# A two-layer image kernel: five statistics tiles asked for first, the next image's statistics two units later, one load of layer 1 behind the last unit's reciprocal

## The chip, the cores and the metric

The kernel runs on one core of one Trainium2 chip. The metric is the device time of one execution in microseconds (us); the median of three runs is shown. A profile is one further execution taken by the hardware profiler. Its engines are PE (TensorE, matmuls; PEld is its weight loads), DVE (VectorE), ACT (ScalarE), POOL (GpSimd) and SP (SyncE). SP and POOL issue the DMA transfers.

## The reference

The input `x` is 2 images of 128 channels, 256 x 256 pixels, f32. Each of two layers adds a branch to its normalised input:

```
x = x + L0(gn(x))     # windowed attention
x = x + L1(gn(x))     # convolutions
gn(v): per image, 32 groups of 4 channels: (v - mean) / sqrt(var + 1e-5)
L0: qkv = W_qkv x; q in 8 x 8 windows, k and v in 12 x 12 windows around them, 4 heads of 32
    softmax(q k / sqrt(32) + relative height and width logits + mask) v, then W_out
    (the mask leaves the keys whose row and column distances are even)
L1: t3 = depthwise 3 x 1 (full 5 x 1 convolution of x)
    t4 = x at columns -2, 0, +2 summed with w4 to 8 channels;   result = t4 * t3
```

The mean and variance of `gn` run over a whole image and four channels, so layer 0 cannot begin before the whole first image has been read once, and layer 1 normalises with statistics of layer 0's result.

## The kernel before

**Statistics of image 0.** `attention_fast` reads image 0 in tiles of 8 rows (1024 KB, name `f_sx`, six buffers) and runs `bn_stats` on VectorE, four per tile (line 128), with `bn_aggr` after every eight tiles (line 136). Three tiles are asked for ahead of the constants (`first = 3`), the first of them in four pieces of 2 rows; then come five constants, `wq_nat` and `relT`, and then the other 27 tiles, each as a buffer comes free (line 302). The last two of the 32 row groups come through `load_rows` as `f_raw` (10 rows, 1280 KB). The mean and the inverse deviation follow, and then the attention begins. Every transfer of SP waits for the eighth before it to have landed, since the transfers share eight completion semaphores in turn.

**Attention.** The work runs in units `u`; a strip `k` is 8 rows of an image (32 strips an image, 64 in all), and each strip has two units, `r` = 0 and 1, for the window rows' two parities: 128 units. A unit issues biases (L591), scores (L608), exponentials (L618), the next unit's keys (L411), coefficients (L502, L511, L515), `attend` (L634, with the reciprocals of line 640 and the products of line 643, three of each), the transposes (L654), values (L524) or the next two units' queries (L474, L476), and the projection (L411), whose result is added to the input (L670) and stored as `x1` (L674). The order in which each engine gets its instructions is the order in which the code is written (`manual_schedule`), across all five engines, SP too. `bring` and `bring_top` copy the new value rows into the window buffers `f_vt` by SP transfers (L554, L558, L561; L571, L575, L578).

**Statistics of image 1** are taken while image 0's attention runs: `stats_at` says in which unit how many rows' `bn_stats` are run, `load_next` asks for the next group of rows at the end of `attend`, behind the first reciprocal of the unit (`seen["output"]`). The one buffer of these rows (`sx`) is also the buffer of `f_top`, the top rows of an image's first strip; `f_top` is read by `bring_top` in unit 0.

**Layer 1** is a generator, `convolutions_fast`. Its first five pieces are called from the attention's last units: at the start of unit 124, at the start of unit 126, after the keys in unit 126, at the start of unit 127, and after `attend` in unit 127. `load_rows1(b, s)` asks for the rows of a strip (640 KB, line 823, and 384 KB of the strip below, line 825). `start_strip` normalises a strip (L836, L839, L840 on ScalarE), `row_sums` makes sums and differences on VectorE (L886, L890), `unfold` makes the 8-channel part (L899, copies L909 and L910, then five small SP transfers L913), `top_row` is `a_first` (L919). After these comes the loop over 64 strips, in which `vertical` (a_c, a_d, a_e, a_o) and the products run.

A load is put behind an instruction by a helper inside `attention_fast`, which adds a dependency by hand.

Of the kernel before, what the change touches and what calls it, by code (L numbers as in the profile page):

```python
# [184 lines left out]
        return self.done[name][:2]  # L185


def attention_fast(tc, io, x1_d, norm, st_x, st_y, tags, ends, weights, both, layer1):

    nc = tc.nc  # L190
    x = io["x"]
    NB, _, H, _ = x.shape
    NS = H // 8
    NU = 2 * NB * NS
    with ExitStack() as l0:
# [42 lines left out]

        raws, norms, qs, cfs, pts, ots, rcs, ons, x1s = ({} for _ in range(9))

        def after(load, ins):
            tc.add_manual_dep(
                load.ins, ins.ins.name,
                mybir.DependencyInfo(mybir.DependencyClass.Sync, mybir.DependencyReason.DATA),
                reason="a load that follows an instruction of the unit",
            )

        def load_rows(k, behind=None):

            b, s = divmod(k, NS)  # L250
            t = rawp.tile([P, 10, W], F32, tag="raw", name=f"f_raw_{k}")
            n = min(10, H - 8 * s)
            load = nc.sync.dma_start(t[:, 0:n, :], x[b, :, 8 * s : 8 * s + n, :])
            if behind:
                after(load, behind)
            raws[k] = t

        with ExitStack() as setup:
            sp = setup.enter_context(tc.tile_pool(name="f_setup", bufs=6))
            first = 3  # L260

            def statistics(i, t):
                norm.chunk(st_x[0], 4 * i, t)
                if i % 8 == 7 and i < NS - 1:
                    norm.quarter(st_x[0], "x0", i // 8)

            ahead = []
            for i in range(first):
                t = sp.tile([P, 8, W], F32, tag="sx", name=f"f_sx_0_{i}")
                for lo in range(0, 8, 8 if i else 2):  # L270
                    hi = lo + (8 if i else 2)
                    nc.sync.dma_start(t[:, lo:hi], x[0, :, 8 * (i + 2) + lo : 8 * (i + 2) + hi, :])
                ahead.append(t)
            for t, src in constants:
                nc.sync.dma_start(t, src)
            nc.scalar.mul(wq_s, wqkvT[:, 0:P], SCALE)
            wq_nat = sp.tile([P, P], F32, tag="wq_nat", name="f_wq_nat", bufs=1)
            nc.sync.dma_start(wq_nat, io["w_q"])
            relT = sp.tile([P, 2 * NREL], F32, tag="relT", name="f_relT", bufs=1)
            nc.sync.dma_start(relT, io["relT"])  # L280
            g_rel = sp.tile([P, HEADS, 2 * NREL], F32, tag="g_rel", name="f_g_rel", bufs=1)
            for h in range(HEADS):
                pg = ps_pj.tile([P, 512], F32, tag="pj", name=f"f_pg_{h}")


                nc.tensor.matmul(
                    pg[:, : 2 * NREL], wq_nat[32 * h : 32 * h + 32, :],
                    relT[32 * h : 32 * h + 32, :], start=True, stop=True,
                )
                nc.scalar.mul(g_rel[:, h, :], pg[:, : 2 * NREL], SCALE)  # L290
            for t in range(4):
                o = 11 - 2 * t
                for t1 in range(4):
                    nc.scalar.copy(wb[:, t, t1, :, 0:6], g_rel[:, :, o : o + 11 : 2])
                o = NREL + 11 - 2 * t
                for t2 in range(4):
                    nc.scalar.copy(wb[:, t2, t, :, 6:12], g_rel[:, :, o : o + 11 : 2])
            for i, t in enumerate(ahead):
                statistics(i, t)
            for i in range(first, NS - 2):  # L300
                t = sp.tile([P, 8, W], F32, tag="sx", name=f"f_sx_0_{i}")
                nc.sync.dma_start(t, x[0, :, 8 * (i + 2) : 8 * (i + 2) + 8, :])
                statistics(i, t)
            for i in range(2):
                load_rows(i)
                statistics(NS - 2 + i, raws[i][:, 0:8])
# [11 lines left out]
        stats_at, norm_at = {}, {}  # L318
        quarter_at = {}
        for b in range(NB - 1):  # L320
            row = 0
            for i in range(NS - 3):
                n = 10 if i < 12 else 8
                stats_at[2 * (b * NS + i) + 2] = b + 1, row, n
                row += n
            for i, u in enumerate((16, 28, 44, 58)):
                quarter_at[2 * b * NS + u] = st_x, b + 1, f"x{b + 1}", i
            last = 2 * (b * NS + NS - 2)
            norm_at[last - 1] = st_x, b + 1, f"x{b + 1}"
            norm_at[last + 10] = st_y, b, f"y{b}"  # L330
# [3 lines left out]
        coming, sxs, seen = sorted(stats_at), {}, {}  # L334

        def load_next():
            if coming:
                u = coming.pop(0)
                b, row, n = stats_at[u]
                t = rawp.tile([P, 10, W], F32, tag="sx", name=f"f_sx_{b}_{row}", bufs=1)  # L340
                sxs[u] = t[:, 0:n]
                after(nc.sync.dma_start(sxs[u], x[b, :, row : row + n, :]), seen["output"])

        def input_stats(u):
            b, row, n = stats_at[u]
# [277 lines left out]
        def attend(u):  # L623
            p = pts.pop(u)
            ons[0] = on = wk.tile([P, 2, NPAIR, 32], F32, tag="on", name=f"f_on_{u}", bufs=1)
            k, r = divmod(u, 2)
            if r == 0:
                rcs[0] = wk.tile([P, 2, NPAIR, 2, 1], F32, tag="rc", name=f"f_rc_{k}")
            for lo, hi in ((0, 6), (6, 11), (11, NPAIR)):
                bank = ps_pj.tile([P, 512], F32, tag="pj", name=f"f_o_{u}_{lo}")  # L630
                po = bank[:, 0 : 66 * (hi - lo)].rearrange("p (n c d) -> p n c d", c=2, d=33)
                for n in range(lo, hi):
                    for h in range(HEADS):
                        nc.tensor.matmul(  # L634
                            po[32 * h : 32 * h + 32, n - lo], p[:, h // 2, n, h % 2],
                            vt[r][:, :, n, h], start=True, stop=True,
                        )

                rc = rcs[0][:, r, lo:hi]
                ins = nc.vector.reciprocal(rc, po[:, :, :, 32:33])  # L640
                if lo == 0:
                    seen["output"] = ins
                nc.vector.tensor_tensor(  # L643
                    on[:, :, lo:hi].rearrange("p c n d -> p n c d"), po[:, :, :, 0:32],
                    rc.to_broadcast([P, hi - lo, 2, 32]), ALU.mult,
                )
# [46 lines left out]
        with tc.manual_schedule(engines=ORDERED):  # L693
# [14 lines left out]
            for u in range(NU):  # L708
                k, r = divmod(u, 2)
                b, s = divmod(k, NS)  # L710
# [5 lines left out]
                if u in norm_at:  # L716
                    st, i, name = norm_at[u]
# [22 lines left out]
                if k % NS == NS - 2:  # L740
                    step()
                attend(u)
                if u == 0 or u in stats_at:
                    load_next()
                if more and r == 1:
                    bring(1, slots_of(k + 1))
# [21 lines left out]
                if u in quarter_at:  # L768
                    st, i, name, part = quarter_at[u]
# [29 lines left out]
def convolutions_fast(tc, io, x1_d, norm, st_y, out, weights, count_good, both):  # L799

    nc = tc.nc
    NB, _, H, _ = io["x"].shape
    NS = H // 8
    with ExitStack() as l1:
# [5 lines left out]
        def rows_buffer(i):  # L810
            t = both.sb.tile([P, 12 * 260], F32, tag=f"x{i}", name=f"xm{i}")
            xn[i] = t.rearrange("p (r w) -> p r w", w=260)
            for side in (0, 2 + W):
                nc.gpsimd.memset(xn[i][:, :, side : side + 2], 0.0)

        def load_rows1(b, s):

            if s == 0:
                pre = rawp.tile([P, 10, W], F32, tag="sx", name=f"raw1_{b}_pre", bufs=1)
                nc.sync.dma_start(pre[:, 5:8, :], x1_d[b][0][:, 0:3, :])  # L820
                raws[b, -1] = pre
            t = rawp.tile([P, 10, W], F32, tag="raw", name=f"raw1_{b}_{s}")
            nc.sync.dma_start(t[:, 0:5, :], x1_d[b][s][:, 3:8, :])
            if s + 1 < NS:
                nc.sync.dma_start(t[:, 5:8, :], x1_d[b][s + 1][:, 0:3, :])
            raws[b, s] = t
# [21 lines left out]
        def pixel_buffers():  # L848

            t = both.sb.tile([P, NPAIR * HEADS * 33], F32, tag="vn", name="t4p")  # L850
            for i in range(2):
                by_pixel.append(
                    t[:, 2 * (W + 4) * i : 2 * (W + 4) * (i + 1)].rearrange("p (r w) -> p r w", r=2)
                )
                for side in (0, 2 + W):
                    nc.gpsimd.memset(by_pixel[i][:, :, side : side + 2], 0.0)
# [8 lines left out]
        def start_strip(k):  # L865
            b, s = divmod(k, NS)
            normalise1(b, s, k, *norm.done[f"y{b}"])
# [202 lines left out]

        load_rows1(0, 0)
        yield
        load_rows1(0, 1)
        yield
        rows_buffer(0)
        start_strip(0)
        yield
        row_sums(0)
        pixel_buffers()
        yield  # L1080
        unfold(0)
        top = top_row(0)
        yield
# [655 lines left out]
```

## Time and profile before

| | us |
|---|---|
| median of 3 runs | 2878.11 (2877.47 to 2878.49) |
| the profiled execution | 2877.88 |
| its span, first to last instruction | 2875.9 |
| statistics of image 0, to the last `bn_stats` | 91.8 |
| first to last unit's biases | 115.15 to 1872.10 |
| loop of layer 1, from a_c of strip 0 | 1884.3 to the end |

| engine | busy us | share |
|---|---|---|
| PE | 2753.5 | 96% |
| DVE | 2134.2 | 74% |
| PEld | 2090.1 | 73% |
| ACT | 1506.2 | 52% |
| POOL | 640.4 | 22% |

In the profile's rows, `out<-in xN` names what an instruction writes and reads and how many there are; "<-" before an engine's or a transfer's name says for what the engine waited, and "issue" is time in which the engine waited for nothing that the profile shows. L12 is line 12 of the kernel. In the chain of work, a row is start, length (both us) and what ran. Queue q8, of kind "instruction", is the transfer of instructions to an engine. Two units, that is one strip, take 27.4 us through most of the attention.

### The profile page before, as it was taken

To read this page: it belongs to the slowest core of one execution; us is meant where nothing else is said; L and a number is where in the kernel's file an instruction comes from. 1 tells how busy PE (TensorE), PEld (TensorE's weight loads), DVE (VectorE), ACT (ScalarE), POOL (GpSimd) and SP (SyncE) were. 2 spreads that over 40 slices of the span, in tenths; PEclk is the share of its full clock that TensorE was granted. 3 is DMA by queue.
4 is the path that set the end of the run, shared out by engine and by line. 5 is a ranking of instruction groups with operands and counts; after the bars stand their busy time and mean duration, and the time that the engine had idled before them with its cause. 6 is when DMAs were issued, how large, how long until landed. Compare 5 with 4: busy or idle time off the path is not lost.

```text
span 2875.9 us, 117447 instructions
## 1 busy us (share of the span) xinstructions
PE 2753.5 (96%) x51762; PEld 2090.1 (73%) x51762; DVE 2134.2 (74%) x3601; ACT 1506.2 (52%) x2379; POOL 640.4 (22%) x2049
## 2 busy tenths in 40 slices
PE   0599999999999999999999999999999999999998
PEld 0489999999999898999999999854444444444444
DVE  8667776776677666566656665589999998999987
ACT  1344454554544545455454554556666656666654
POOL 1223323333333333333333333200000000000000
PEclk9999999999999999999999999999999999999999
DMA  9566666666666455555554455557888888888885
GB/s 390 170 189 184 194 172 183 189 165 186 178 171 165 127 149 134 143 141 133 140 141 134 140 137 144 136 153 215 215 215 220 219 214 213 218 219 212 218 217 147
DMA packets 157988, 519.74 MB, mean 181 GB/s; under 512 B 20800, under 2 KB 98080, under 8 KB 117536
## 3 DMA queue, kind: packets, MB, share of 16 engines
q1 hardware_dynamic: 148400, 446.07, 52.6%
q0 software_dynamic: 9072, 66.06, 12.3%
q8 instruction: 412, 6.75, 0.9%
q14 instruction: 104, 0.85, 0.1%
HBM read 282.68 MB, written 134.22 MB: 145 GB/s over the span
## 4 chain that ended last, share of the span: by engine, by line
PE 79%; issue 17%; POOL 1%; DMA 1%; ACT 1%; DVE 1%; SPq 0%; POOLq 0%; ACTq 0%; DVEq 0%
PE f_s L608 10%; PE f_o L634 9%; PE f_pk L411 8%; PE f_pv L524 8%; PE f_py L411 8%; PE a_o L919 6%; PE a_e L919 6%; PE f_pq L476 6%; PE f_pa L502 5%; PE f_s L591 5%; PE f_pq L474 2%; PE a_d L970 2%; PE a_c L919 1%; PE b L1012 1%; PE g L899 1%
## 5 line engine op out<-in xcount | busy, mean ns | idle before, releaser
L515 DVE TENSOR_SCALAR f_cf<-f_pa,f_keep 128x512 f32<-128x512 f32 x128 | 103.7, 810 | 539.8 <-ACT f_cf L511 539.7
L618 ACT ACTIVATE f_p<-f_s 128x512 f32<-128x512 f32 x512 | 264.4, 603 | 403.1 <-PE f_s L608 403.0
L482 ACT ACTIVATE f_q<-f_pq,f_head 128x512 f32<-128x512 f32 x512 | 303.1, 702 | 146.8 <-PE f_pq L476 146.8
L425 POOL COPY f_kt<-f_kt 128x60 f32<-128x60 f32 (+1 forms) x348 | 105.7, 340 | 1176.8 <-ACT f_kt L439 1153.1
L994 ACT ACTIVATE t<-t,w 128x1024 f32<-128x1024 f32 x127 | 145.9, 1149 | 368.0 <-DVE t L987 362.8
L402 POOL COPY f_xq<-f_xn 128x96 f32<-128x96 f32 x1024 | 333.8, 357 | 3.3 <-DVE f_xn L385 3.3
L1001 DVE SCALAR_TENSOR_TENSOR t<-t,w,t 128x1024 f32<-128x1024 f32 x254 | 326.0, 1283 | 7.3 <-ACT t L994 1.3
L608 PEld LDWEIGHTS f_s<-f_q,f_kt 64*64 64x64 f32 x17176 | 270.4, 133 | 49.5 <-issue 49.5
L608 PE MATMUL f_s<-f_q,f_kt 64*64 64x64 f32 (+1 forms) x17176 | 288.1, 221 | 0.1
L634 PE MATMUL f_o<-f_vt,f_p 128*32 128x66 f32 x16384 | 263.6, 220 | 3.4 <-issue 3.4
L1030 POOL DMA_DIRECT2D y<-f_x x63 | 54.5, 866 | 919.2 <-DVE y L1022 871.2
L411 PE MATMUL f_pk<-f_xn,f_wqkvT 128*128 128x192 f32 (+3 forms) x1496 | 258.1, 322 | 0.7 <-ACT f_kt L439 0.7
L634 PEld LDWEIGHTS f_o<-f_vt,f_p 128*32 128x32 f32 x16384 | 241.8, 108 | 12.9 <-issue 2.0
L919 PE MATMUL a_o<-xm,w1s 128*128 128x512 f32 x512 | 242.3, 595 | 4.6 <-ACT t L910 4.6
L524 PE MATMUL f_pv<-f_wqkvT,f_xn 128*128 128x128 f32 x2048 | 246.0, 279 | 0.6 <-DVE f_cf L515 0.3
L411 PE MATMUL f_py<-f_ot,f_woT 128*128 128x160 f32 (+1 forms) x1520 | 244.5, 311 | 2.0 <-DVE f_ot L654 1.8
L919 PE MATMUL a_e<-xm,w1s 128*128 128x512 f32 x512 | 240.8, 591 | 0.0
L524 PEld LDWEIGHTS f_pv<-f_wqkvT,f_xn 128*128 128x128 f32 x2048 | 233.7, 192 | 6.7 <-DVE f_cf L515 0.5
L411 PEld LDWEIGHTS f_py<-f_ot,f_woT 128*128 128x128 f32 x1520 | 228.3, 191 | 4.2 <-issue 3.7
L411 PEld LDWEIGHTS f_pk<-f_xn,f_wqkvT 128*128 128x128 f32 x1496 | 221.5, 190 | 12.5 <-issue 1.7
L476 PE MATMUL f_pq<-f_xn,f_wq_s 128*128 128x192 f32 (+1 forms) x1008 | 210.4, 331 | 0.0
L643 DVE TENSOR_TENSOR f_on<-f_o,f_rc 128x320 f32<-128x320 f32 (+1 forms) x384 | 197.2, 514 | 13.3
(150 smaller groups left out, 4660.5 us busy)
## 6 DMA issues: line engine op xcount, KB each, us to landing
f_raw<-in_x SPq DMA_DIRECT2D x62, 1280.0 KB
f_x<-f_x SPq DMA_DIRECT2D x128, 512.0 KB
y<-f_x POOLq DMA_DIRECT2D x63, 1024.0 KB, 7.9
out<-y SPq DMA_DIRECT2D x63, 1024.0 KB
f_sx<-in_x SPq DMA_DIRECT2D x46, 1024.0 KB
f_vt<-f_vn SPq DMA_DIRECT2D x172, 264.0 KB
raw<-f_x SPq DMA_DIRECT2D x64, 640.0 KB
raw<-f_x SPq DMA_DIRECT2D x62, 384.0 KB
```

Of the source, the lines that this page charges most:

```text
L402: nc.gpsimd.tensor_copy(xq[:, half, t2, 1:4, :, c].rearrange("p t r n e -> p r t n e"), xn[k % 2][:, windows, :, c, 0:3, t2:8:4].rearrange ...
L411: nc.tensor.matmul(dst[:, 512 * lo // last : 512 * hi // last], w, moving[:, n * lo // last : n * hi // last], start=True, stop=True,)
L476: nc.tensor.matmul(by_pair[:, lo:hi, 8:32], wq_s, xn[k % 2][:, lo:hi, r, c, 0:3].rearrange("p n i j -> p n (i j)"), start=True, stop=True,)
L482: nc.scalar.activation(q[:, c, :, i].rearrange("p n (j t) -> p n j t", t=4), pq.rearrange("p (n t j) -> p n j t", n=NPAIR, t=4), AF.Copy, ...
L524: nc.tensor.matmul(pv[:, P * n : P * n + P], xn[k % 2][:, 4 * g + n].rearrange("p r c i j -> p (r c i j)"), wvT, start=True, stop=True,)
L608: nc.tensor.matmul(sc[g][n // 8][64 * c : 64 * c + 64, n % 8, lo:hi].rearrange("p i x -> p (i x)"), kt[r][rows, c, NKEY * n : NKEY * n + 6 ...
L618: seen["exp", half, g] = nc.scalar.activation(pts[u][:, g, 8 * half : 8 * half + 8].rearrange("p n i x -> p (n i x)"), sc[g][half].rearran ...
L634: nc.tensor.matmul(po[32 * h : 32 * h + 32, n - lo], p[:, h // 2, n, h % 2], vt[r][:, :, n, h], start=True, stop=True,)
L643: nc.vector.tensor_tensor(on[:, :, lo:hi].rearrange("p c n d -> p n c d"), po[:, :, :, 0:32], rc.to_broadcast([P, hi - lo, 2, 32]), ALU.mult,)
L919: nc.tensor.matmul(pa[:, : n * W], w, rows, start=i == 0, stop=i == len(terms) - 1)
L994: nc.scalar.activation(t3[:, j : j + 4], t1[:, j : j + 4, :], AF.Copy, scale=w3[:, 0:1])
L1001: nc.vector.scalar_tensor_tensor(t3[:, j : j + 4], t1[:, j + tap : j + tap + 4, :], w3[:, tap : tap + 1], t3[:, j : j + 4], ALU.mult, ALU.add,
```

## The change

There are three parts. (1) Five tiles instead of three are asked for ahead of the constants, and the first comes in two pieces of 4 rows instead of four of 2. (2) The statistics of the next image begin in unit 4 instead of unit 2; there are 28 groups of rows instead of 29, and sixteen of 10 rows instead of twelve; the first load is asked for in unit 2 instead of unit 0. The last unit with statistics stays unit 58. (3) In layer 1's lead-in, the second strip's rows are asked for in the fifth piece, after `attend` of unit 127, with a dependency on that unit's first reciprocal, and no longer in the second piece; `rows_buffer(0)` (memsets on POOL) goes to the second piece, and `start_strip(0)` is alone in the third. By the built program's order, the third strip's rows move on SP from ahead of `unfold(0)`'s transfers to behind the last `x1` store. The order on TensorE and ScalarE is unchanged; on POOL two edge copies of keys go behind the memsets.

```
+def follow(tc, load, ins):
...
-            first = 3
+            first = 5
...
-                for lo in range(0, 8, 8 if i else 2):
-                    hi = lo + (8 if i else 2)
+                for lo in range(0, 8, 8 if i else 4):
+                    hi = lo + (8 if i else 4)
...
-            for i in range(NS - 3):
-                n = 10 if i < 12 else 8
-                stats_at[2 * (b * NS + i) + 2] = b + 1, row, n
+            for i in range(NS - 4):
+                n = 10 if i < 16 else 8
+                stats_at[2 * (b * NS + i) + 4] = b + 1, row, n
...
-                    seen["output"] = ins
+                    seen["output"] = weights.output = ins
...
-                if u == 0 or u in stats_at:
+                if u == 2 or u in stats_at:
                     load_next()
...
-        def load_rows1(b, s):
+        def load_rows1(b, s, behind=None):
...
-            nc.sync.dma_start(t[:, 0:5, :], x1_d[b][s][:, 3:8, :])
+            load = nc.sync.dma_start(t[:, 0:5, :], x1_d[b][s][:, 3:8, :])
+            if behind:
+                follow(tc, load, behind)
...
         load_rows1(0, 0)
         yield
-        load_rows1(0, 1)
+        rows_buffer(0)
         yield
-        rows_buffer(0)
         start_strip(0)
         yield
         row_sums(0)
         pixel_buffers()
         yield
+        load_rows1(0, 1, weights.output)
         unfold(0)
         top = top_row(0)
         yield
```

More of the change, by code (lines that the diff above doesn't have):

```diff
@@ L185, in group @@
         return self.done[name][:2]
+def follow(tc, load, ins):
+    tc.add_manual_dep(
+        load.ins, ins.ins.name,
+        mybir.DependencyInfo(mybir.DependencyClass.Sync, mybir.DependencyReason.DATA),
+        reason="a load that follows an instruction of the unit",
+    )
 def attention_fast(tc, io, x1_d, norm, st_x, st_y, tags, ends, weights, both, layer1):
@@ L239, in attention_fast @@
         raws, norms, qs, cfs, pts, ots, rcs, ons, x1s = ({} for _ in range(9))
[L241 to L246, printed above, removed]
         def load_rows(k, behind=None):
@@ L254, in load_rows @@
             if behind:
-                after(load, behind)
+                follow(tc, load, behind)
             raws[k] = t
@@ L341, in load_next @@
                 sxs[u] = t[:, 0:n]
-                after(nc.sync.dma_start(sxs[u], x[b, :, row : row + n, :]), seen["output"])
+                follow(tc, nc.sync.dma_start(sxs[u], x[b, :, row : row + n, :]), seen["output"])
         def input_stats(u):
@@ L822, in load_rows1 @@
             t = rawp.tile([P, 10, W], F32, tag="raw", name=f"raw1_{b}_{s}")
-            nc.sync.dma_start(t[:, 0:5, :], x1_d[b][s][:, 3:8, :])
+            load = nc.sync.dma_start(t[:, 0:5, :], x1_d[b][s][:, 3:8, :])
+            if behind:
+                follow(tc, load, behind)
             if s + 1 < NS:
```

## The prediction

> **What bounds the kernel now.** I read the page first, then TensorE's waits, the chain of work around each wait, the DMA queue's issues there, and VectorE's order in the first 92 us.
>
> ```profile
> PE 2753.5 (96%) x51762; PEld 2090.1 (73%) x51762; DVE 2134.2 (74%) x3601; ACT 1506.2 (52%) x2379; POOL 640.4 (22%) x2049
> q8 instruction: 412, 6.75, 0.9%
> ```
>
> TensorE is the bound once it starts, so a change pays only in the first 92 us, before TensorE has work, or where TensorE stands still. The second line matters later: TensorE's instructions arrive by DMA. 6.75 MB in 412 packets is 16.4 KB a packet, and 2 x 51762 records over 412 packets is 251, so a packet is a page of about 256 instructions.
>
> The waits of TensorE from 115 to 215 us, and the chain there (start, us, what; unit 1, then unit 3):
>
> ```profile
> PE f_pq L474 <- issue: 4.9, 1, 4.9
> ```
> ```profile
> 139.20 0.42 PE f_pq L474 x2
> ...
> 141.25 4.86 issue
> 146.10 0.58 PE f_pq L474
> 146.68 1.28 PE f_pq L476 x2
> ...
> 152.07 1.05 PE f_s L591 x32
> ...
> 174.04 0.42 PE f_pq L474 x2
> ...
> 179.47 1.05 PE f_s L591 x32
> ```
>
> From its first f_pq to the next unit's f_s, unit 1 takes 12.87 us and unit 3, with the same work, 5.43. The 7.44 us between them are 4.86 of standing and 2.58 of slow matmuls: L476 takes 1.28 for 0.65, and the granted clock is 0.50 from 145 to 150 us. "issue" names no engine. I counted TensorE's records up to its four gaps over 1 us after 115 us caused by "issue": 960, 1728, 97472 and 98240 stand before them. Divided by 256 each leaves 192, so each gap opens exactly where a page ends. The page missing in unit 1 left as a q8 packet at 143.34, took 1.32, and work resumed 1.44 after its end. TensorE had entered the page before at 137.26, and I take that as the moment of the request: 6.08 us of waiting. For the 360 pages inside the attention loop the same wait is 1.36 at the median, 0.55 to 2.1 for nine in ten, 2.93 at most. What lay in the way:
>
> ```profile
> 136.67 0.33 SPq L342 DMA_DIRECT2D f_sx<-in_x  x1
> ...
> 140.96 1.08 SPq L674 DMA_DIRECT2D f_x<-f_x  x1
> 145.78 0.57 SPq L554 DMA_DIRECT2D f_vt<-f_vn  x1
> ```
>
> The 1280 KB of next-image rows asked for at 136.67 (they had waited for f_top, and keep SP waiting until 145.78) start 0.6 us ahead of the request. At the layer boundary the chain shows the same twice:
>
> ```profile
> 1865.58 1.73 issue
> ...
> 1876.10 0.55 issue
> ...
> 1880.06 1.68 issue
> ```
>
> Layer 1's second rows (1024 KB) are asked for at 1860.78, and the page requested at 1861.58 waits 3.35; the third rows at 1873.90, and the page requested at 1875.88 waits 3.54.
>
> **Part 1, five tiles first.** VectorE, start and us:
>
> ```profile
> 10.40 5.04 DVE L128 BATCH_NORM_STATS2 f_st_x<-f_sx 128x6 f32<-128x512 f32 x8 [1.94 <-DMA f_sx<-in_x]
> 17.67 12.42 DVE L128 BATCH_NORM_STATS2 f_st_x<-f_sx 128x6 f32<-128x512 f32 x20 [2.24 <-DMA f_sx<-in_x]
> ```
>
> It looks as if 2.24 us could be had. But sx 3 is late because its request waits for sx 2 to land (12.96): SP's transfers share eight semaphores in turn. After the change sx 5 waits for sx 4 in the same way, so the gap moves two tiles on. From 15 to 85 us the DMA engines are full (share 1.01, 424 GB/s, 2.48 us a tile) while VectorE needs 4 x 0.595 = 2.38 plus 1.0 for every eighth tile, 2.50. So the transfers set the end at 89.31. They lose time in 13 to 15 us (155 GB/s), a hole that only moves, and in the first tile, whose 2 KB pieces ran at 305 to 334 KB/us against 418 later. Two pieces of 4 rows for four of 2 recover at most 1.05 MB x (1/320 - 1/418) = 0.8 us; a slow start of any transfer recovers nothing. VectorE's first wait (4.16) grows by about 1 us, covered by later ones. I take -0.6, between -2.2 (the 2.24 gap wins after all) and +0.8 (sx 5 half a microsecond later, its VectorE lead used up). The moved constants arrive some 3 to 5 us later; their work on ScalarE ends at 20 us and the next thing that needs it, f_pa, runs at 108, so cost zero, covered by 80 us.
>
> **Part 2, statistics from unit 4.** The load at 136.67 and five bn_stats in unit 2 go; the five groups at units 26 to 34 grow by one bn_stats each (0.61) and from 1024 to 1280 KB. That is VectorE work under TensorE's 27.4 us for two units, of which VectorE uses about 20: zero, and if the cover were gone 2.4 us. The load now issued in unit 2 stands where before's second load stands (160.12), and loads of 1280 KB at units 4 to 24 left no gap at TensorE. SP also loses the 1.3 us wait for f_top and the 3.7 us wait before 145.78, so unit 3's six f_vt transfers go about 4 us earlier; they are needed at 172. The late page then waits like the others: 1.36 + 0.95 (packet) + 1.44 against the 3.71 us that its predecessor takes to run, a gap of 0.04; with 2.1 it is 0.8. I take 0.3. The half clock goes with the gap. Sum: -7.44 + 0.3 = -7.1, from -7.4 to -2.4.
>
> [...]
>
> **Part 3, the second strip's rows.** The 1024 KB leave 1860.78 and are asked for behind the reciprocal at 1877.46; the third strip's rows now come behind the last x1 store (1885.26). The memsets go one step earlier on POOL, which idles 12.2 us ahead of them; the edge copies of the last keys (L425, 1865.11) now queue behind them, and 0.9 us of memsets done by then cost nothing. The first late page needs 1.36 + 0.93 + 1.45 against 3.78: gap 0, I allow 0.3, so -1.4. The second, likewise, -1.5; its request at 1875.88 is 1.6 us ahead of the moved load. The 0.55 stays: that page ran in 2.41 us. What the wait holds up on SP: the five L913 copies (1880.62) and the last x1 store, both later than the reciprocal anyway. Who waits for the rows: ScalarE's L839 (1886.24, in the new time 1884.7). The third rows in before, 1024 KB asked for at 1873.90 behind a 512 KB store, left the DMA engines quiet at 1879.4; the same 5.5 plus 1 for landing puts the second rows at 1884.1, 0.6 us in time, and ScalarE has 1.3 more before VectorE's L886. Beyond that a microsecond late costs one, since VectorE runs from there almost without a break (one of 0.44) to L987, for which a_c waits. Part 3: -2.9, from -3.4 to +4.
>
> **Sum.** -0.6 - 7.1 - 2.9 = -10.6 on the profiled execution, 2877.88 us with a span of 2875.9: 2867.3. That execution is 0.23 below the median of 2878.11, so 2867.5 in its terms. Layer 1 is TensorE's own (its busy digits in the page's slices are 9 almost to the end), so an earlier start carries through.
>
> **Rivals.** (A) The unit 1 page stays partly late, behind f_vt copies and the x1 store, which come earlier too: a gap of 2.5 and the half clock again (2.5) leave -2.4 of 7.4; total -5.9, 2872. For it: that store is asked for 2 us earlier. Against: other units have both and wait 2.93 at most. (B) The moved load meets the page requested at the boundary: with 6.08 of waiting the gap is 6.08 + 0.98 + 1.4 - 3.81 = 4.65 for 1.68, with half clock +5.5, total about -3.6: 2874.5. For it: 1024 KB behind the reciprocal, close to the request; against: the request is ahead. (C) The loads are not the cause and nothing moves but the start: 2877.5. (D) Slower: pages wait behind the short packets of f_vt, not behind rows. Then the gap stays, and the f_vt transfers of unit 3, 4 us earlier, delay the next page (requested about 141) as well: one more gap with half clock, +7.4, nothing from part 3, -0.6: 2885. It ends slower once the new gap costs over 0.6. Against it: sixty odd units have these packets without a gap.
>
> **Chances.** Forecast 0.76 (own range 2864.5 to 2870.5), A 0.12, B 0.06, C 0.02, D 0.04. About 0.2%, 5.8 us, is what a measurement here can tell from no change. Faster: the forecast and three quarters of A, 0.85; same: the rest of A, B and C, 0.11; slower: D, 0.04. The range runs from 2864 (start -2.2, no residue: -12.7, and a little) to 2872.5 (A).
>
> **What would show it.** Right: no "issue" wait near 141, unit 1 about 13.7 us long, clock 1.00 there; L839 on the second strip not waiting for a DMA; the two gaps at the boundary under 0.5; VectorE's late first tile at sx 5, and raw 1 landing near 88.7. Wrong: a gap of over 2 us at a page's end in units 1 to 2 or after the last reciprocal, or VectorE waiting over 1 us again between 25 and 85 us.

## The result, and the profile after

The changed kernel takes 2867.48 us (median of 9 runs, 2865.58 to 2870.22) and the kernel before 2878.11 us (9 runs, 2872.55 to 2880.53). The ratio is 0.9965, with a 95% interval of 0.9954 to 0.9975: 10.1 us faster by the ratio, between 7.2 and 13.2. The forecast was 2867.5. The profiled execution of the changed kernel took 2865.81 us, with a span of 2863.9.

The chain of work of the changed kernel, in unit 1 and at the layer boundary (start, us, what):

```profile
139.46 0.11 PE f_pq L476
139.57 0.54 issue
140.11 0.38 PE f_pq L476
...
143.74 1.05 PE f_s L593 x32
...
1865.94 0.82 issue
...
1869.55 0.63 PE a_first L923 x2
1870.21 1.02 PE a_first L923 x4
1871.23 1.74 PE f_py L413 x12
```

The gap of 4.86 us in unit 1 is now 0.54, the granted clock is 1.00 from 138 to 144 us, and of the three gaps at the boundary one is left (0.82, for 0.55). VectorE's row in the first 92 us:

```profile
9.28 9.95 DVE L128 BATCH_NORM_STATS2 f_st_x<-f_sx 128x6 f32<-128x512 f32 x16 [1.31 <-DMA f_sx<-in_x]
21.40 7.43 DVE L128 BATCH_NORM_STATS2 f_st_x<-f_sx 128x6 f32<-128x512 f32 x12 [2.18 <-DMA f_sx<-in_x]
...
90.57 1.02 DVE L136 BATCH_NORM_AGGREGATE mv_x<-f_st_x 128x2 f32<-128x192 f32 x1
```

The wait of 2.24 us has become one of 2.18 two tiles later, now for tile 5. From 25 us to the end of the statistics VectorE then waits 0.7 us at most at a time. The last aggregate starts at 90.57; before, it started at 91.81:

```profile
91.81 1.02 DVE L136 BATCH_NORM_AGGREGATE mv_x<-f_st_x 128x2 f32<-128x192 f32 x1
```

Taken from one span to the other, the two profiled executions differ by 12.1 us in these places, each read as the distance from one unit's first f_s (biases) to the next one's:

| stretch | before | after | difference |
|---|---|---|---|
| start to the biases of unit 0 | 115.15 | 113.45 | -1.70 |
| unit 0 | 15.84 | 15.77 | -0.07 |
| unit 1 | 21.01 | 14.45 | -6.56 |
| units 2 to 125 | 1707.24 | 1707.26 | +0.02 |
| unit 126 | 12.86 | 11.01 | -1.85 |
| unit 127 and layer 1 | 1003.85 | 1001.93 | -1.92 |

The five larger groups of rows in units 26 to 34 cost nothing that shows: 124 units agree to 0.02 us in all. Each column is one execution; units 1 and 126 vary from one to the next, as the experiments show.

### The profile page after: what moved, and what is told of

It reads as the page before. It is cut to its first block, busy times and chain, and to the rows that moved or that the text cites. A ratio compares the mean times of both kernels' runs of the same rounds, so it can differ in the third digit from the quotient of the medians.

```text
span 2863.9 us, 117440 instructions
## 1 busy us (share of the span) xinstructions
PE 2749.8 (96%) x51762; PEld 2086.8 (73%) x51762; DVE 2133.8 (75%) x3601; ACT 1506.7 (53%) x2379; POOL 642.8 (22%) x2049
## 4 chain that ended last, share of the span: by engine, by line
PE 79%; issue 17%; DMA 1%; POOL 1%; ACT 1%; DVE 1%; SPq 0%; POOLq 0%; ACTq 0%; DVEq 0%
PE f_s L610 10%; PE f_o L636 9%; PE f_pk L413 8%; PE f_pv L526 8%; PE f_py L413 8%; PE a_o L923 6%; PE a_e L923 6%; PE f_pq L478 6%; PE f_pa L504 5%; PE f_s L593 5%; PE f_pq L476 2%; PE a_d L974 2%; PE a_c L923 1%; PE b L1016 1%; PE g L903 1%
```

## The experiments

**Each half of the page argument alone.** `e1_part2` is the kernel before with part 2 alone.

```
-            for i in range(NS - 3):
-                n = 10 if i < 12 else 8
-                stats_at[2 * (b * NS + i) + 2] = b + 1, row, n
+            for i in range(NS - 4):
+                n = 10 if i < 16 else 8
+                stats_at[2 * (b * NS + i) + 4] = b + 1, row, n
...
-                if u == 0 or u in stats_at:
+                if u == 2 or u in stats_at:
```

> Part 2 alone: the next image's statistics from unit 4, first load in unit 2, all else as before. Theory (the 1280 KB asked for at 136.67 us hold up an instruction page of TensorE): unit 1 takes 14.5 us instead of 21.0 with no half clock near 144 us, all other units as before; time -6.5, about 2871.5. Rival (the pages wait behind the f_vt packets or for something that the move does not touch): unit 1 still near 21 us, 2878.

Measured: 2874.4 us for 2878.78 (ratio 0.9986, 0.9978 to 0.9994), 4.0 to 4.4 us faster. Unit 1 takes 14.18 us, and there is no half clock near 144 us. TensorE's wait at f_pq from 115 to 165 us in this kernel:

```profile
PE f_pq L474 <- issue: 0.3, 1, 0.3
```

The place is the expected one and the rival falls; the gain is 2 us short of what was expected. The profile shows something else that had been taken as fixed. The boundary is that of before, and yet its first late page now costs 3.10 us, where it cost 1.73 in the profile of before:

```profile
1859.08 3.10 issue
```

A half clock of 6.83 us follows, which the boundary of before did not have, and unit 126 takes 16.56 us for 12.86. In the four profiles with that boundary and those page ends (before, this one, `e3_small_load` and `e9_full_page`) unit 126 takes 12.86, 16.56, 14.25 and 13.81 us: the profile of before has the shortest. In the six profiles in which the rows wait for the reciprocal it takes 11.01 to 11.27.

`e2_part3` is the changed kernel with parts 1 and 2 undone, so that part 3 is alone.

```
-            first = 5
+            first = 3
...
-                for lo in range(0, 8, 8 if i else 4):
-                    hi = lo + (8 if i else 4)
+                for lo in range(0, 8, 8 if i else 2):
+                    hi = lo + (8 if i else 2)
...
-            for i in range(NS - 4):
-                n = 10 if i < 16 else 8
-                stats_at[2 * (b * NS + i) + 4] = b + 1, row, n
+            for i in range(NS - 3):
+                n = 10 if i < 12 else 8
+                stats_at[2 * (b * NS + i) + 2] = b + 1, row, n
...
-                if u == 2 or u in stats_at:
+                if u == 0 or u in stats_at:
```

> Part 3 alone: the second strip's rows behind the reciprocal, parts 1 and 2 undone. Theory: the two page gaps at the layer boundary (1.73 and 1.68 us) go, unit 126 takes 11.0 us instead of 12.9, time -3 to -3.7, about 2874.7; unit 1 keeps its 21.0 us. Rival (the gain at the boundary came from the earlier memsets or from an earlier start of the units): unit 126 stays near 12.9 and the time at 2878.

Measured: 2875.41 us for 2878.78 (ratio 0.9986, 0.998 to 0.9993), 3.4 us faster by the medians and 4.0 by the ratio. Unit 126 takes 11.01 us and the wait at a_first is 0.3 us for 1.7. Unit 1 still has its gap, but a smaller one than in the profile of before:

```profile
PE f_pq L476 <- issue: 2.9, 1, 2.9
```

Unit 1 takes 18.41 us here, and only 3.4 us of half clock follow. In the third profile of a kernel whose unit 1 is that of before (`e9_full_page`, below) it takes 19.25. So the 21.01 us of the first profile were the largest of three.

**Bytes, or the wait on SP.** `e3_small_load` leaves the first load in unit 0, with its wait for f_top and its place, and takes 8 of its 10 rows away; other groups take them up.

```
+            sizes = [2] + [10] * 15 + [8] * 13
             for i in range(NS - 3):
-                n = 10 if i < 12 else 8
+                n = sizes[i]
```

> Kernel before with the first group of next-image rows cut from 10 rows to 2 (256 KB for 1280 KB), the other 28 groups take up the rest. The load stays in unit 0, keeps its wait for f_top and its place on SP; only its bytes go. Theory (bytes in front of the page): the page requested at 137 us waits about 2 us, unit 1 takes 14 to 15 us, time -6, about 2872. Rival (the wait for f_top on SP, which bunches the f_vt transfers, or the f_vt packets themselves): unit 1 stays near 21 us, 2878.

Measured: 2874.21 us for 2878.78 (ratio 0.9985, 0.9978 to 0.9992), as much as part 2 gives. Unit 1 takes 13.86 us. Its chain:

```profile
140.87 0.11 PE f_pq L475
140.98 0.04 issue
141.03 0.38 PE f_pq L475
```

The wait for f_top is as long as before, 1.3 us, and the gap is gone. But the load also goes out earlier here, at 133.15 us for 136.67, since SP waited less ahead of it, and the f_vt transfers move with it. What separates bytes from time is `e9_full_page` (below), which has the whole 1280 KB and sent them at nearly the same moment. SP's issue in `e3_small_load`, then in `e9_full_page`, and the wait of TensorE in the latter:

```profile
133.15 0.33 SPq L343 DMA_DIRECT2D f_sx<-in_x  x1
```
```profile
133.72 0.33 SPq L343 DMA_DIRECT2D f_sx<-in_x  x1
```
```profile
PE f_pq L475 <- issue: 3.8, 1, 3.8
```

The page was asked for at 137.0 and 136.9 us, taken as in the prediction as the moment at which TensorE enters the page before; its q8 packet left 1.67 us later behind 256 KB, and 5.01 us later behind 1280 KB. So it was the bytes. Rival D of the prediction, pages behind the f_vt packets, is out: those packets stand close around the request in both.

**Where the pages end.** `e4_page_shift` adds 32 matmuls, 128 records of TensorE, to the first 25 us, where TensorE otherwise waits. `e9_full_page` adds 64 matmuls, 256 records. Both write the same product again and again. The diff is that of `e4_page_shift`; `e9_full_page` has 17 for 9.

```
-                nc.tensor.matmul(
-                    pg[:, : 2 * NREL], wq_nat[32 * h : 32 * h + 32, :],
-                    relT[32 * h : 32 * h + 32, :], start=True, stop=True,
-                )
+                for _ in range(9):
+                    nc.tensor.matmul(
+                        pg[:, : 2 * NREL], wq_nat[32 * h : 32 * h + 32, :],
+                        relT[32 * h : 32 * h + 32, :], start=True, stop=True,
+                    )
```

> Kernel before with each of the four small set-up matmuls (L286) issued nine times instead of once: 32 more matmuls, 128 more records of TensorE in the first 25 us, where it is otherwise idle. Nothing else changes, but every page of 256 instructions ends 128 records earlier in the work. Theory (gaps are late pages): gaps still open where the count of records leaves 192 when divided by 256, so in other work than before: none at the f_pq of unit 1; the page that the load at 136.67 us holds up is wanted some 3.5 us later, in the scores of unit 2, and the gap shrinks to 0 to 2 us, time -4 to -7 there. Rival (f_pq waits for a buffer or another engine): the gap of 4.9 us stays at f_pq, time 2878.

Measured: 3193.76 us, 11% slower than before (ratio 1.1099, 1.108 to 1.1118). The expectation for unit 1 holds (14.78 us, no gap at f_pq). That for unit 2 does not: a gap of 0 to 2 us was expected in the scores, and 3.72 us stand in f_o. And I had given no thought to the other 400 pages. TensorE's waits over the whole execution:

```profile
PE f_o L635 <- issue: 208.9, 114, 4.2
...
PE f_pk L412 <- issue: 12.9, 28, 1.1
```

and the chain in unit 2, one of many:

```profile
150.63 1.50 PE f_o L635 x90
152.12 3.72 issue
155.85 0.78 PE f_o L635 x38
156.62 3.41 PE f_pv L525 x16
```

I counted the records ahead of every stretch of over 0.7 us between two starts of TensorE's records from 115 us to 2750 us. There are 119, and 116 of them leave 192 when divided by 256, the same rest as in before, with 128 records more in front. So the gaps stand in other work than before and still at the ends of pages.

The records also tell why there are so many. From the request of a page to TensorE's resuming, a page needs about 3.75 us, an estimate from the prediction's figures (1.36 to leave, 0.95 to come, 1.44 until TensorE resumes). I took the time in which TensorE runs through each of the 357 pages between the biases of units 2 and 121, from its first record to its last. In before the shortest takes 3.99 us and the median is 4.43, so the next page is there in time. With half a page of shift the work is cut elsewhere, and some pages hold short instructions alone: 195 of the 357 run in under 3.7 us, the shortest in 2.18. 109 of these pages end in a gap of over 0.7 us, all 109 among the 195. The wait of a page before it leaves is the same at the median, 1.35 us against the prediction's 1.36. In `e9_full_page` the shortest is 3.99 us again.

The standing of 209 + 13 us, of which before had some 10, and the slower matmuls (TensorE's busy time is 2861.9 us for 2753.5, with a mean clock of 0.978) come to about 320 us; the span grew by 309.5.

> Kernel before with each set-up matmul issued seventeen times: 64 more matmuls, 256 more records, one whole page, where the shift by half a page (128 records) took 3193.8. Theory (the place of the page ends in the work decides): the page ends fall on the same work as before, 2878 plus or minus 5. Rival (more set-up work or more instructions cost by themselves): slower than 3193, or at least far above 2878.

Measured: 2878.33 us for 2877.89 (ratio 1.0002, 0.9995 to 1.0009). Twice the extra matmuls cost nothing, since a whole page puts every end back on the same work. Together the two runs show that it is the place of the page ends, and not the number of instructions.

**Does the rows' load need the wait on the reciprocal?** `e5_no_wait` is the changed kernel without it.

```
-        load_rows1(0, 1, weights.output)
+        load_rows1(0, 1)
```

> Changed kernel without the dependency on the last reciprocal: the second strip's rows keep their new place in the code and so come on SP right behind unit 126's x1 store, some 4 us earlier than with the wait, and the first half of the third strip's rows follows them. Theory (a load in front of a page's request delays it): the page wanted in a_first is late again, a gap of 1 to 3 us there, time +1 to +3 against the changed kernel, about 2869.5. Rival (it is enough that the rows leave the start of unit 126): no new gap, 2867.5.

Measured: 2873.2 us (ratio to before 0.9985, 0.9979 to 0.9992), 5.7 us above the changed kernel. The rows are now asked for at 1864.05 us, behind unit 126's store, and 640 KB of the third strip's rows at 1866.65. The chain, and then the windows from 1870 us (TensorE's clock is the number after the five engines):

```profile
1870.19 0.63 PE a_first L923 x2
1870.82 4.69 issue
1875.51 1.87 PE a_first L923 x4
1877.37 3.13 PE f_py L413 x12
```
```profile
1870.00:1876.00 6.00, 1.31 (x8) 0.89 (x5) 3.36 (x8) 1.07 (x2) 0.00 (x0) 0.77 0.50 167
1876.00:1880.00 4.00, 4.00 (x14) 3.73 (x13) 0.69 (x1) 0.37 (x1) 0.00 (x0) 0.50 0.00 0
```

TensorE stands for 4.69 us and a half clock of 6.83 us follows. The page was asked for at 1867.40 us and left 5.67 us later. The direction was right, the size was not: the gap was expected at 1 to 3 us, and the half clock had been left out. What is not told apart is the share of the second strip's rows and of the third's, which the removal also brings forward. In the changed kernel the rows come at 1867.84, 3.8 us later and 1.1 us behind the request of that page, which leaves 1.15 us after it is asked for.

**Part 1 taken apart.** `e6_pieces` is the changed kernel with three tiles ahead of the constants, `e7_five` the changed kernel with pieces of 2 rows.

```
-            first = 5
+            first = 3
```
```
-                for lo in range(0, 8, 8 if i else 4):
-                    hi = lo + (8 if i else 4)
+                for lo in range(0, 8, 8 if i else 2):
+                    hi = lo + (8 if i else 2)
```

> Changed kernel with three tiles ahead of the constants again; the first still in two pieces of 4 rows. Read is the start of the last statistics aggregate on VectorE (91.81 us before, 90.57 in the changed kernel). Theory (larger pieces use the transfers better, the five tiles only move the hole): about 90.7. Rival (the five tiles are the gain): about 91.8.

> Changed kernel with the first tile in four pieces of 2 rows again, five tiles still ahead of the constants. Read is the start of the last statistics aggregate on VectorE (91.81 us before, 90.57 in the changed kernel, 90.19 with three tiles and 4-row pieces). Theory (the pieces are the gain, the five tiles only move the hole): 91.5 to 92.4, as in kernels with three tiles and 2-row pieces. Rival (five tiles gain on their own): below 91.2.

The last aggregate of `e6_pieces`, and then of `e7_five`:

```profile
90.19 1.02 DVE L136 BATCH_NORM_AGGREGATE mv_x<-f_st_x 128x2 f32<-128x192 f32 x1
```
```profile
92.47 1.02 DVE L136 BATCH_NORM_AGGREGATE mv_x<-f_st_x 128x2 f32<-128x192 f32 x1
```

Over the profiles of this study, the aggregate starts at 91.69 to 92.41 us with three tiles and 2-row pieces (six kernels), at 92.47 with five tiles and 2-row pieces, at 90.19 and 90.66 with three tiles and 4-row pieces, and at 90.57 to 90.83 with five tiles and 4-row pieces (three kernels). The pieces are worth about 1.4 us, the five tiles nothing that shows; `e7_five` lies 0.07 us above the range expected for it. The single times were 2864.52 and 2869.55 us; one run each settles nothing beyond this reading.

**A version that beats both.** The profile after has one large wait of TensorE left, 4.6 us at a_o behind ScalarE. ScalarE waits there for a matrix whose load was issued 6.4 us ahead. TensorE's wait, and then the load and ScalarE's row in the timeline (the bracket is its wait):

```profile
PE a_o L923 <- ACT t L914: 4.6, 1, 4.6
```
```profile
2785.40 1.05 SPq L953 DMA_DIRECT2D ident<-in_c_ident  x1
...
2791.79 0.98 ACT L956 ACTIVATE dg<-ident,w 128x128 f32<-128x128 f32 x3 [6.06 <-DMA ident<-in_c_ident]
```

`e8_ident` asks for it one strip earlier; `identity` holds the tile and its load, taken out of `diagonals`.

```
-                if k + 4 == NB * NS:
-                    dg = diagonals()
+                if k + 5 == NB * NS:
+                    ident = identity()
+                if k + 4 == NB * NS:
+                    dg = diagonals(ident)
```

> Changed kernel with the identity matrix of layer 1's last strips asked for one strip earlier (in strip 59, with the scaling on ScalarE left in strip 60). In the changed kernel ScalarE waits 6.1 us for that load, and a_o waits 4.6 us for ScalarE and then runs at half clock for 6.8 us. Theory: TensorE's wait of 4.6 and some 2.5 of half clock go, time -6 to -7 against the changed kernel, about 2860.8. Rival (the end is set by the transfers of the last strips): no change, 2867.5.

Measured: 2860.13 us (ratio to before 0.9938, 0.9922 to 0.9955), 7.4 us below the changed kernel. The wait of a_o is gone from the list of TensorE's waits, and the clock is 1.00 there. One figure of the expectation is that of the kernel before: a half clock of 6.8 us follows the wait there, while in the profile of the changed kernel it lasts 3.41.

`e10_both` adds the three tiles of `e6_pieces` to it.

> Changed kernel with the identity matrix asked for one strip earlier and three tiles instead of five ahead of the constants. Theory (five tiles gain nothing): the same as with the early identity alone, 2860.1 plus or minus 1. Rival (the five tiles gain): slower than 2861.5.

Measured: 2861.66 us (2860.83 to 2862.43) for 2860.13 (2858.73 to 2860.32) of `e8_ident`, which falls just past the rival's bound. But the kernel before took 2878.43 us beside the one and 2877.89 beside the other. Against it the ratios are 0.994 and 0.9938, with intervals that overlap nearly whole, so this is no difference clear of noise. The aggregate starts at 90.66, against 90.83 there, so nothing is lost in the statistics; in its profile TensorE waits 0.9 us for a page at f_pq in unit 1 and 0.6 us at a_first, where it waits 0.2 and 0.3 us in that of `e8_ident`. Whether the number of tiles has to do with those is open. It gives no reason to call the five tiles a gain.

## Why the prediction was right

The mechanism was right. That the total was met to the microsecond is luck: its terms were off by up to 2.7 us, and their errors cancel in part.

- **The mechanism, pages of instructions behind row loads**: right, and shown from three sides. Fewer bytes at the same moment remove the gap (0.04 us behind 256 KB in `e3_small_load`, 3.8 behind 1280 KB in `e9_full_page`); half a page of shift moves the gaps to other work and a whole page moves none (3193.76 us in `e4_page_shift`, 2878.33 in `e9_full_page`); loads a few microseconds earlier bring a gap back (4.69 us in `e5_no_wait`).
- **Where TensorE stops**: counted from 115 to 2750 us, stretches of over 0.7 us between two starts of its records stand at 5 of the 406 page ends of 256 records in before (0.76 to 5.12 us), at 3 of the 407 in the changed kernel (0.81 to 1.29) and at 116 in the shifted kernel. At the other page ends no stretch is that long.
- **Part 2, -7.1**: measured -4.4 alone (1.7 to 6.3 by the interval). The term that was mis-sized is the 7.44 us read off one execution. The three profiles with that unit show 21.0, 18.4 and 19.3 us, 5.5 us on average above the 14.1 us that it takes in the seven profiles in which the load is moved (13.55 to 14.73). The residue was sized at 0.3 from the median wait of 1.36; the page waited 2.04 and the gap was 0.54.
- **Part 3, -2.9**: measured -3.4 alone (2.0 to 5.8 by the interval), with both gaps gone. This term too was read off one execution, here the one with the shortest unit 126, and it has no half clock in it, which three of the four profiles with that boundary show. Rival B's price, a gap of 4.65 us with half clock, is what `e5_no_wait` shows (4.69, +5.7 us) when the load is not held behind the reciprocal. The strip's rows came in time: ScalarE's L843 started at 1874.71 with no wait of its own.
- **Part 1, -0.6**: read from profiles alone, -1.2 in the pair and -1.4 over all; it was not timed by itself. That five tiles only move the hole was right. The gain of larger pieces was capped at 0.8 from the first tile alone; in the trace the tile behind it also ran faster, 414 to 426 KB/us between 6 and 8 us for 334 to 352. The start is 1.70 us shorter to the biases of unit 0; 1.24 of that is the statistics.
- The parts add up to 1.4 + 4.4 + 3.4 = 9.2 us, against 10.1 to 10.6 together, which is within the intervals.
- **Rival A**, part of the gap staying in unit 1, holds in a small way (0.54 us, 0.9 in one other profile). C and D are out by `e1_part2` and `e3_small_load`.

## What to carry to other kernels

Where TensorE stands still with nothing released ("issue"), count its instructions up to the gap: here the gaps whose count leaves 192 when divided by 256 were late instruction pages. What helped was to keep large loads away from the moments at which a page is asked for (behind 256 KB it left 1.67 us later, behind 1280 KB 5.01). An edit that adds instructions early moved every later page end here, and its effect on the time was far larger than its own cost: 128 records more made the kernel 11% slower. That a shift can also make a kernel faster as a whole was not shown. Pad to a whole page before judging such an edit (256 records more cost nothing here), and look for pages that run faster than the next one can come (195 of 357 in under 3.7 us in the shifted kernel). Read a stall off more than one execution before putting its length in a sum.

## What was not expected

- 128 records more in an idle stretch of TensorE cost 315 us (3193.76 for 2878.78), and 256 cost none (2878.33 for 2877.89).
- After a wait of 2.9 us TensorE's clock was one half for 3.4 us (`e2_part3`), but the length of the wait does not settle how much comes. After the wait of a_o it was one half for 6.83 us in the profile of before (4.60 us long) and for 3.41 in that of the changed kernel (4.62); after a wait of 2.73 us in `e9_full_page` no half clock came. The stretches of half clock start at 144.06, 2803.04 and 2871.31 us in the profile of before and at 2793.76 and 2862.02 in that of the changed kernel. The distances are 2658.98, 68.27 and 68.26 us, which is 779, 20 and 20 times 3.4133. Apart from the one at the end of the span they last 6.83, 6.83 and 3.41 us. What sets their starts and lengths was not shown.
- With the first tile asked for in pieces of 4 KB a channel instead of 2 KB, the transfer rate was higher not only in that tile (305 to 334 KB/us between 3 and 5 us before, 311 to 373 in the changed kernel, 365 to 377 in `e6_pieces`) but in the tile behind it (334 to 352 between 6 and 8 us before, 414 to 426 in the changed kernel).
